# Layer 3 of a four-layer recurrent kernel: where the second pair's projections stand, and where the routing's one-hot rows live

## The chip, the cores and the metric

The kernel runs on one core of a Trainium2 chip (trn2), as a single program. The metric is the device time of one execution in microseconds (us); before the change the median of four runs is 1407.51 us (1401.19 to 1417.63). All arithmetic is fp32. The engines are named as the profile names them: PE (TensorE, matrix products), DVE (VectorE), ACT (ScalarE), POOL (GpSimd), and SP, which here only issues DMAs.

## The reference

The model has four layers. Each takes `x` (2 x 1024 tokens, 128 channels), normalises it, computes a mixer `s` and a mixture of experts `g` from the same normalised rows `xn`, and adds `s * silu(g)`:

```
xn = _layernorm(x)
s = _L3_attn_ref(xn, ...)          # two Mamba2 scans, one per direction, 64 channels each
g = _silu(_L3_ffn_ref(xn, ...))    # 16 experts of width 64, the best 2 per token, and a shared expert
x = x + s * g
```

Only layer 3 is touched. Its mixer runs a Mamba2 block forwards on the first 64 channels and one backwards on the last 64:

```
zxbcdt = u @ in_w.T
z, xBC, dt = ...
xBC = silu(conv4(xBC) + conv_b)                  # x, B and C, 128 columns each
dt = softplus(dt + dt_bias); dA = exp(-exp(A_log) * dt)
h = dA_t * h + outer(dt_t * x_t, B_t);  y_t = h @ C_t      # over 1024 steps, two heads of 64
y = rmsnorm((y + D * x) * silu(z)) * gnorm_w;  out = y @ outp_w.T
mixer(x) = x + concat(out_f, out_b) @ op_w.T + op_b        # here x is the layer's xn
```

Its experts choose, for each token, the two highest of 16 logits, weigh them by a softmax over the two, and add `down(silu(gate(xn)) * up(xn))` of the chosen two and of a shared expert.

## The kernel before

**Tiles.** The 2048 tokens are 16 tiles of 128 (`NT`), in four groups of four tiles (`NG`, `G`). `x`, `xn` (token rows) and `xT` (channel rows) stay in on-chip memory through the whole kernel. Layer 3 opens memory pools of its own: `pa` for the mixer, `pf` for the experts, `e3` for what comes after the routing, and eight PSUM banks, four for the mixer (`sa`) and four for the experts (`sf`).

**The mixer, `StateSpace`.** The scan is cut into chunks of 128 steps, and four chunks (512 tokens) of one direction are a *unit*. A forward and a backward unit are worked on together as a *pair*; there are four pairs. For each unit `stacked` makes the projections with the convolution folded in: three `px` (x, B, C; two matmuls of 128x512 accumulated in one bank each) that ACT turns into `uxs` by a Silu (line 473), and one `pz` that becomes `usz` (line 483). `xs` and `sz` have four buffers each, so two pairs' projections fit at once. `unit` then does the scan: decay matrices (`uda` on DVE or POOL, `pd` on PE, an exponential to `uE` on ACT, line 559), `pe`, the transposes `pt`, `pcb`, the states `pst`, then `py` and `pi`, the row norm (`pss`, `ur`) and the output product `pyo`, which `gated` (line 1736) adds into the tile `s0`. Between the two, `steps` makes the step sizes and decays for all tokens (a softplus on DVE with one exponential on ACT, line 344; then `pc` and the exponential of line 450).

**The experts.** `top2` finds the two experts of each token on DVE. The class `Dispatch` then works out, mostly on DVE, for each of 47 blocks of 128 rows which tokens go there: `pr` (a count by matmul), prefix sums, and at the end a list made by 32 small matmuls `pinv` of two kinds of one-hot rows: `dla`, made four tiles at a time in two buffers, and `dhh`, one tile of 128 x 1536 that DVE compares (line 1205) and POOL multiplies by the slot numbers (line 1206). The list gives `dfrom` and `dto`, for the gather of rows (line 1231) and the scatter of results (line 1241), both issued by POOL. The 47 blocks are worked on in twelve groups of four: gather `xb`, transpose `pxb`, `pgb`, Silu, `hb`, transpose `phb`, `pob`, copy to `yb`, scatter into `ys`. `xb` has two buffers, and the weights `tw` (issued by SP) three.

**The end.** When all scatters have landed, `fetch` reads `ys` back (`yt`) and DVE adds the rows to `acc` (line 409), which holds the shared expert's output (`pgt`, `put`, `hT`, `psh`). Then a Silu, the product with `s0`, the sum into `x`, and the store.

**What sets the order.** The program text gives an order of writing: normalisation, `top2`, `Dispatch`, `stacked` of pair 0, `steps`, units of pair 0 together with `stacked` of pair 1, the twelve expert groups, the shared expert, then for pairs 1 to 3 the units together with the next pair's `stacked`, then the end. The framework does not keep to it: it places the instructions on each engine by a timeline of its own (`schedule_with_timeline_sim=True`), in which what is written earlier has precedence. Each engine then works strictly in its own order and waits on semaphores. So one moved statement can move instructions of the experts on all engines.

**Where the one-hot rows live before.** `Dispatch` is given a place for `dhh`: a buffer of the tag `uxs` in `pa`, of 1536 elements, the first of the four that the projections use later. With pair 0 in the next two, the backward unit of pair 1 comes round to the buffer that held `dhh`.

Of the kernel before, what the change touches and what calls it, by code (L numbers as in the profile page):

```python
# [10 lines left out]
F32 = mybir.dt.float32  # L11
# [8 lines left out]
P = 128  # L20
NB, SEQ = 2, 1024
T = NB * SEQ
NT = T // P
# [630 lines left out]
def together(*parts):  # L654

    live = list(parts)
    while live:
        live = [p for p in live if next(p, p) is not p]
# [1000 lines left out]
def layer3(K, x, xn, xT, w, inp, out):  # L1659
    nc, tc, c = K.nc, K.tc, K.c  # L1660
    four = [P, G, P]
    with ExitStack() as es:
        pa = es.enter_context(tc.tile_pool(name="a3", bufs=1))
        pf = es.enter_context(tc.tile_pool(name="f3", bufs=1))
        sa = es.enter_context(tc.tile_pool(name="sa3", bufs=4, space=PSUM))
        sf = es.enter_context(tc.tile_pool(name="sf3", bufs=4, space=PSUM))
# [55 lines left out]
        with tc.tile_pool(name="r3", bufs=1) as pr:  # L1722
            lg = pr.tile([P, NT, 16], F32, name="lg")
            nc.vector.tensor_add(lg, pl[:, :, :16], w["br"].unsqueeze(1).to_broadcast([P, NT, 16]))
            pdt = pa.tile([P, NT, 4], F32, name="pdt")
            nc.vector.tensor_mul(pdt, pl[:, :, 16:], rs.unsqueeze(2).to_broadcast([P, NT, 4]))
            (m1, h1), (m2, h2) = K.top2(pr, lg, 16)
            d = Dispatch(K, pf, pr, sf, h1, h2, 16, P, inp["lists"], ((pa, "uxs", 4, 1536), (pa, "uda", 2)))
            w12 = K.pair_softmax(pf, m1, m2)
        pe = es.enter_context(tc.tile_pool(name="e3", bufs=1))  # L1730
        s0 = pa.tile([P, NT, P], F32, name="s")
        for g in range(NG):
            nc.gpsimd.tensor_add(grp(s0, g), grp(xn, g), w["opb"].unsqueeze(1).to_broadcast(four))

# [12 lines left out]
        space = StateSpace(K, pa, sa, parts)  # L1747
        pairs = [[(m, b, n) for m in parts] for b in range(NB) for n in range(TPB // G)]
        together(space.stacked(pairs[0]))
        space.steps(pdt)  # L1750
        together(*(space.unit(*u, busy=True) for u in pairs[0]), space.stacked(pairs[1]))
        loaded = {}

        def load_rows(n0):
# [5 lines left out]
        for n0 in range(0, d.n, 4):  # L1760
# [29 lines left out]
            K.copy(yb, po)  # L1790
            for r, n in enumerate(part):
                d.store(yb[:, r, :], n)
        acc = pe.tile([P, NT, P], F32, name="acc")
        for g in range(NG):
            rhs = xT[:, g * 512 : (g + 1) * 512]
            pgt = sf.tile([P, 512], F32, name="pgt", tag="ps")
# [21 lines left out]
def build(tc, io, packs):  # L1818
    nc = tc.nc
    with ExitStack() as ctx:  # L1820
        pool = ctx.enter_context(tc.tile_pool(name="const", bufs=1))
        x = pool.tile([P, NT, P], F32, name="x")
        src = io["x"].rearrange("b (t p) d -> p (b t) d", p=P)
        for g in range(NG):
            nc.sync.dma_start(grp(x, g), src[:, g * G : (g + 1) * G, :])
        xn = pool.tile([P, NT, P], F32, name="xn")
        xT = pool.tile([P, T], F32, name="xT")

        def load(into, n, by=nc.scalar):
            t = into.tile([P, packs[n].n], F32, name="w_" + n)  # L1830
            by.dma_start(t, io[n])
            return View(t, packs[n])

        K = Kern(tc, load(pool, "c"))
        dram = ctx.enter_context(tc.tile_pool(name="lists", bufs=1, space=DRAM))
        lists = {n: dram.tile([rows, P], F32, name=n) for n, rows in (("xs", T), ("ys", 2 * T))}
        views = {}
        with tc.tile_pool(name="const0", bufs=1) as pool0:
            w0 = load(pool0, "l0")
            e0 = load(pool0, "e0")  # L1840
            layer0(K, x, xn, xT, w0, e0)
        later = ctx.enter_context(tc.tile_pool(name="const3", bufs=1))
        views["l3"] = load(later, "l3")
        pair = lists["xs"], lists["ys"]
        with tc.tile_pool(name="const2", bufs=1) as pool0:
            views.update((n, load(pool0, n)) for n in ("l1", "l2"))
            layer1(K, x, xn, xT, views["l1"], {"rows": io["rows1"], "lists": pair, **{n: io[n] for n in ("sw1", "sw3", "sw2")}})
            layer2(K, x, xn, xT, views["l2"], {"rows": io["rows2"], "lists": pair})
        layer3(K, x, xn, xT, views["l3"], {"load": lambda pool: load(pool, "x3", nc.sync), "rows": io["rows3"], "lists": pair}, io["out"].rearrange("b (t p) d -> p (b t) d", p=P))
# [17 lines left out]
```

## Time and profile before

| what | us |
|---|---|
| median of 4 runs | 1407.51 (1401.19 to 1417.63) |
| the profiled execution, its own time | 1406.37 |
| its span | 1404.6 |
| busy in the span: PE, DVE, ACT, POOL | 1150.5, 878.0, 633.9, 430.9 |
| layer 3, from its first normalisation to the end of the span | about 1122 to 1404.6 |
| of which routing, until the list is ready | about 1152 to 1186 |
| pair 0, pair 1, pair 2 (from the first `pd` to the last `pyo`) | 1186 to 1245, 1245 to 1302, 1302 to 1351 |
| pair 3, the fetch and the end | 1351 to 1404.6 |

The median and the profiled execution differ by 1.1 us, and the four runs lie within 16.4 us of each other. In the views, a row of the timeline or the chain has the start in us from the span's start, then the duration, then the engine and what it writes; "issue" is time in which an engine waited for nothing that the profile shows. A PE row counts hardware passes: one fp32 matmul of the program is two of them. PEclk is the granted TensorE clock, 1.00 for full speed.

### The profile page before, as it was taken

What the parts mean: (1) busy time and instruction counts of PE and PEld (TensorE: products, weight loads), DVE (VectorE), ACT (ScalarE), POOL (GpSimd) and SP (SyncE); (2) the same over time, 40 slices, a digit from 0 to 9 for tenths busy, and PEclk for the clock granted to TensorE, in tenths of its full rate; (3) what the DMA queues carried; (4) which work ended last, traced back from release to release, by engine and by line L of the source; (5) the groups of instructions that cost most, each with busy time, mean ns of one, the idle gap of its engine ahead of it and who ended that gap; (6) DMA issues with size and microseconds to landing.
All of it is one profiled execution on the core that took longest, in us unless ns stands there. A gap on an engine that the chain in (4) does not pass through costs nothing. (4 is left out here: it accounts for less than half of the span.)

```text
span 1404.6 us, 19123 instructions
## 1 busy us (share of the span) xinstructions
PE 1150.5 (82%) x6813; PEld 801.4 (57%) x6813; DVE 878.0 (63%) x2169; ACT 633.9 (45%) x1051; POOL 430.9 (31%) x424
## 2 busy tenths in 40 slices
PE   5599776797997568999998997699999467887985
PEld 2276455796996335544444432377787344666674
DVE  6536336955754776777777635986673586434456
ACT  7656916116312241445556575225522243463561
POOL 0352260036555240000000000156575222655643
PEclk9799986889999776899999898889999767978997
DMA  2000003113443200000000000133345311222411
GB/s 87 0 1 1 0 15 119 46 43 122 133 132 100 60 1 0 1 1 1 1 1 16 8 1 8 74 83 113 127 133 153 95 58 53 69 62 82 56 51 45
DMA packets 49039, 75.71 MB, mean 54 GB/s; under 512 B 7335, under 2 KB 36402, under 8 KB 48688
## 3 DMA queue, kind: packets, MB, share of 16 engines
q1 hardware_dynamic: 39632, 54.30, 12.2%
q0 software_dynamic: 8448, 14.98, 4.6%
q10 hardware_dynamic: 864, 5.21, 1.0%
q8 instruction: 54, 0.88, 0.3%
q14 instruction: 41, 0.34, 0.1%
HBM read 63.95 MB, written 12.85 MB: 55 GB/s over the span
## 5 line engine op out<-in xcount | busy, mean ns | idle before, releaser
L1458 DVE TENSOR_REDUCE mx<-pm 128x1 f32<-128x512 f32 (+3 forms) x304 | 182.1, 656 | 65.6 <-PE pm L287 63.3
L1502 ACT ACTIVATE pr<-psc 128x1024 f32<-128x1024 f32 x144 | 139.5, 1021 | 94.8 <-PE psc L287 61.3
L1231 POOL DMA_INDIRECT xb<-xs,dfrom x132 | 132.5, 1004 | 150.7 <-PE pxb L808 30.9
L1241 POOL DMA_INDIRECT ys<-yb,dto x132 | 135.9, 1030 | 85.1 <-DVE yb L1119 33.5
L1206 POOL TENSOR_TENSOR dhh<-dhh,w_c 128x1280 fp32r<-128x1280 f32 (+2 forms) x3 | 8.7, 2915 | 474.3 <-DVE dhh L1205 474.3
L287 PE MATMUL pm<-kT,qT 32*128 32x128 f32 (+3 forms) x576 | 119.9, 367 | 16.3 <-DVE mx L1458 12.4
L287 PEld LDWEIGHTS pm<-kT,qT 32*128 32x128 f32 x576 | 69.6, 205 | 69.3 <-DVE mx L1458 49.3
L287 PE MATMUL p<-xbT,tw 128*128 128x256 f32 x368 | 103.1, 397 | 6.8 <-ACT sg L1112 2.4
L1112 ACT ACTIVATE sg<-p,tw 128x256 f32<-128x256 f32 x92 | 41.0, 473 | 100.3 <-PE p L287 85.8
L287 PE MATMUL pat<-pr,va 128*32 128x512 f32 x576 | 82.1, 637 | 0.2 <-ACT pr L1502 0.2
L293 PE MATMUL tp<-w_c,xn 128*128 128x128 f32 x64 | 19.5, 425 | 70.7 <-DVE xn L328 43.5
L287 PEld LDWEIGHTS p<-xbT,tw 128*128 128x128 f32 x368 | 63.8, 196 | 18.9 <-issue 6.4
L1113 DVE SCALAR_TENSOR_TENSOR hh<-p,tw,sg 128x256 f32<-128x256 f32 x92 | 42.6, 478 | 42.8 <-ACT sg L1112 22.0
L287 PE MATMUL psc<-qT,kT 32*128 32x512 f32 x288 | 64.3, 491 | 2.9 <-ACT pr L1502 2.7
L287 PEld LDWEIGHTS po<-tw,hh 128*128 128x128 f32 x368 | 54.3, 192 | 9.0 <-issue 2.2
L287 PE MATMUL po<-tw,hh 128*128 128x128 f32 x368 | 56.3, 277 | 1.0 <-DVE hh L1113 0.6
L293 PEld LDWEIGHTS tp<-w_c,xn 128*128 128x128 f32 x64 | 11.8, 191 | 78.7 <-DVE xn L328 27.8
L287 PE MATMUL psc<-mT,onesR 32*128 32x512 f32 x288 | 54.0, 415 | 0.0
L282 ACT COPY xbT<-pxb 128x256 f32<-128x256 f32 (+3 forms) x39 | 15.6, 400 | 66.2 <-PE pxb L808 34.9
L287 PEld LDWEIGHTS psc<-qT,kT 32*128 32x128 f32 x288 | 30.3, 188 | 15.9 <-ACT pr L1502 13.7
L287 PE MATMUL pd<-uda,w_c 128*128 128x512 f32 x64 | 38.4, 706 | 0.9 <-ACT usz L528 0.9
L556 POOL TENSOR_TENSOR uda<-w_c,vdA 128x512 f32<-128x512 f32 x20 | 20.9, 1053 | 55.4 <-PE pd L287 54.7
(529 smaller groups left out, 2851.1 us busy)
## 6 DMA issues: line engine op xcount, KB each, us to landing
tw<-in_rows SPq DMA_DIRECT2D x23, 836.0 KB
tw<-in_rows SPq DMA_DIRECT2D x39, 384.0 KB
yt<-ys SPq DMA_DIRECT2D x24, 256.0 KB
tw<-in_rows SPq DMA_DIRECT2D x47, 128.0 KB
xb<-xs,dfrom POOLq DMA_INDIRECT x132
ys<-yb,dto POOLq DMA_INDIRECT x132
xs<-xn SPq DMA_DIRECT2D x8, 256.0 KB
w_l<-in_l ACTq DMA_DIRECT2D x1, 1890.0 KB
```

Source lines behind the costliest of these rows:

```text
L282: self.nc.scalar.copy(out, in_)
L287: self.nc.tensor.matmul(out, lhsT=lhsT, rhs=rhs, start=start, stop=stop)
L293: self.nc.tensor.transpose(pt[:, j, :], src(g * G + j), self.c["ident"])
L556: pool.tensor_mul(da, upto.unsqueeze(1).unsqueeze(1).to_broadcast(lay), m["dA"][:, i0 + j : i0 + j + per, :].unsqueeze(3).to_broadcast(lay))
L1112: nc.scalar.activation(sg, p1[:, k - k0, :], AF.Silu, bias=t[:, 1536 + k : 1537 + k])
L1113: nc.vector.scalar_tensor_tensor(hh[:, k, :], p2[:, k - k0, :], t[:, 1540 + k : 1541 + k], sg, ALU.add, ALU.mult)
L1206: nc.gpsimd.tensor_mul(h, h.bitcast(F32), c["slot"][:, at].unsqueeze(2).to_broadcast(shape))
L1231: self.K.nc.gpsimd.indirect_dma_start(dst, None, self.xs, bass.IndirectOffsetOnAxis(self.of_token[:, n : n + 1], 0))
L1241: d = self.K.nc.gpsimd.indirect_dma_start(self.ys, bass.IndirectOffsetOnAxis(self.to[:, n : n + 1], 0), src, None, bounds_check=2 * T - 1, ...
L1458: nc.vector.tensor_reduce(mx[:, starts.index(a), g, j : j + k], tile[0][:, : k * m].rearrange("p (j m) -> p j m", m=m), AX.X, ALU.max)
L1502: K.nc.scalar.activation(pr, ps, AF.Exp, scale=scale)
```

## The change

Four edits, all in `layer3`:

```diff
-            d = Dispatch(..., ((pa, "uxs", 4, 1536), (pa, "uda", 2)))
+            d = Dispatch(..., ((pa, "acc", 1, T), (pa, "uda", 2)))
...
-        s0 = pa.tile([P, NT, P], F32, name="s")
+        s0 = xn
         for g in range(NG):
             nc.gpsimd.tensor_add(grp(s0, g), grp(xn, g), w["opb"].unsqueeze(1).to_broadcast(four))
...
         together(space.stacked(pairs[0]))
+        together(space.stacked(pairs[1]))
         space.steps(pdt)
-        together(*(space.unit(*u, busy=True) for u in pairs[0]), space.stacked(pairs[1]))
+        together(*(space.unit(*u, busy=True) for u in pairs[0]))
...
-        acc = pe.tile([P, NT, P], F32, name="acc")
+        acc = pa.tile([P, NT, P], F32, name="acc", tag="acc")
```

The projections of pair 1 are written right behind those of pair 0 and ahead of `steps`, instead of side by side with the units of pair 0. All four buffers of `uxs` then belong to the projections, and `dhh` gets a tile of its own, of 2048 elements, under the tag `acc`; the same tile later holds the experts' sum `acc`, which moves from the pool `e3` to `pa`. To make room, the separate tile `s` goes: the output bias is added to `xn` in place (POOL, line 1733), and the units add their output to `xn`. The arithmetic is the same.

More of the change, by code (lines that the diff above doesn't have):

```diff
@@ L1727, in layer3 @@
             (m1, h1), (m2, h2) = K.top2(pr, lg, 16)
-            d = Dispatch(K, pf, pr, sf, h1, h2, 16, P, inp["lists"], ((pa, "uxs", 4, 1536), (pa, "uda", 2)))
+            d = Dispatch(K, pf, pr, sf, h1, h2, 16, P, inp["lists"], ((pa, "acc", 1, T), (pa, "uda", 2)))
             w12 = K.pair_softmax(pf, m1, m2)
         pe = es.enter_context(tc.tile_pool(name="e3", bufs=1))
-        s0 = pa.tile([P, NT, P], F32, name="s")
+        s0 = xn
         for g in range(NG):
```

## The prediction

> **What bounds the kernel now.** I read the page, then the chain of work that ended last, the busy times by window, and the engines' own timelines for layer 3. Layers 0 to 2 keep their order, so only 1122 to 1404.6 us counts. The chain through the routing:
>
> ```profile
> 1150.71 22.93 issue
> ...
> 1173.68 3.15 POOL dhh L1206
> ...
> 1176.88 1.90 PE pinv L287 x8
> 1178.78 1.72 PE pc L287 x8
> 1180.50 5.36 PE pinv L287 x24
> ...
> 1185.88 3.75 PE pd L287 x4
> ```
>
> The chain waits 22.9 us for the routing's list of small DVE operations, then goes over POOL's `dhh` and PE's `pinv`. Windows of all engines (columns: PE, weight load, DVE, ACT, POOL busy, then the granted clock, DMA share, GB/s):
>
> ```profile
> 1158.00:1167.00 9.00, 8.81 (x24) 3.57 (x22) 7.54 (x39) 5.56 (x9) 0.00 (x0) 1.00 0.00 0
> 1167.00:1177.00 10.00, 0.12 (x1) 0.12 (x1) 9.86 (x21) 2.21 (x3) 3.14 (x1) 0.70 0.26 77
> 1177.00:1186.00 9.00, 8.98 (x41) 8.78 (x41) 5.32 (x9) 0.28 (x1) 0.00 (x0) 0.50 0.30 91
> ```
> ```profile
> 1186.00:1220.00 34.00, 33.10 (x154) 20.76 (x156) 15.45 (x34) 17.89 (x25) 20.91 (x20) 0.92 0.19 52
> 1220.00:1245.00 25.00, 17.03 (x109) 15.80 (x110) 9.42 (x24) 9.12 (x13) 14.49 (x16) 0.68 0.27 79
> ```
>
> PE stands idle for 10 us while DVE ends the routing, and is full (33.1 of 34) right after it. That is the place the change aims at: pair 1's projections stand in the full stretch and would go into the idle one. Their share of it, by the same view for `px` alone:
>
> ```profile
> 1186.00:1220.00 34.00, 12.02 (x24) 4.91 (x24) 0.00 (x0) 4.12 (x6) 0.92 0.19 52
> ```
>
> In the chain `px` takes 4.45 (1189.63), 3.44, 1.72 and 1.72 us, and `pz` 1.09: **12.4 us**, all on the path.
>
> **The change, part by part.** The sum is made against the profiled execution's own 1406.4 us; the median of the runs, 1407.5, lies 1.1 above it.
>
> *1. The routing gets later, its list shorter.* The built program's order puts pair 0's first Silu ahead of the softplus exponential `spe` on ACT. Before:
>
> ```profile
> 1153.25 1.28 ACT L344 ACT_TABLE_LOAD   x1
> 1155.02 0.26 ACT L344 ACTIVATE spe<-spe 128x64 f32<-128x64 f32 x1 [0.49 <-DVE spe L343]
> 1158.12 0.22 ACT L385 ACTIVATE rd<-rd 128x16 f32<-128x16 f32 x1 [2.85 <-DVE rd L384]
> 1158.36 1.28 ACT L473 ACT_TABLE_LOAD   x1
> ```
>
> Now `spe` waits for the first `px` (its row ends at 1156.3), a Silu (0.69) and a table load (1.28): it ends at 1156.4 + 0.7 + 1.3 + 0.3 = 1158.7 instead of 1155.3. Behind it on DVE waits line 345, and behind that all of `top2` and `Dispatch`; one reduction (0.42) now stands ahead, so DVE loses 2.9 us. The other exponential, `rd`, then stands behind a load, two Silus and a load (1.28 + 1.38 + 1.28 + 0.22): 1162.9, where DVE would want it at 1158.7 + 3.3 = 1162.0: 0.9 more. With five operations left to it (1.2 to 1.6), `dbo` ends near 1164.3, 4.1 late. The 2.1 us that DVE then waited for `pr` are filled now: step-size operations that stood among the prefix sums (lines 354, 444, 562: 0.9) run in that wait. That leaves `dhh` 3.2 late: `pinv` can begin at 1180, not 1176.9. The list itself gets shorter. `pc` (1.72) no longer cuts into it, because the new order has `pc` ahead. And at a granted clock of 1.00 its 32 matmuls (7.26 us at 0.50) are paced by six `dla` of 0.69 with a gap of 0.16: 5.1 + 0.5 = 5.6. End: 1185.6 at full clock, 1187.3 at half, against 1185.9. I take **+0.5**; bounds -2 (no exponential late) to +12 (rival two).
>
> A rule speaks against this part. The Trainium skill (ScalarE: Activation LUTs, "What ACT_TABLE_LOAD costs") puts a switch of tables at about 2.66 us, 1.28 for the load and 1.38 to drain. In this trace the Silu at 1194.18 ends at 1194.87, the load starts at 1194.89 and the exponential at 1196.18, so a switch costs 1.3 here. By the page's figure, an estimate, the three switches that now stand before `rd` would add 4 us to the routing.
>
> *2. Unit pair 0 loses 12.4 us of PE work.* Between `pinv`'s end (T0 = 1185.9) and the first `py` (1219.96) lie 34 us. What is late next is the first gather: POOL's four issues start 1.2 us after T0, stand 1.3 apart, and `pxb` now meets them with nothing but three `pd` (2.6 us at full clock) in front, so about 3 us of the hiding that `px` gave is lost; the rows are there at T0 + 5.6 (first two) and T0 + 8.8 (all). Then `xbT` and `uwide` on DVE (1.2), `pe` 0.9, `pt` and `pgb` with `pt` 2.7, `pcb` 1.8: T0 + 15.5. From `pcb` to `py` DVE decides: products, `hb`, `ucb`, `uE`, states, some 6.5 us: **T0 + 22 instead of T0 + 34, so -12**. From `py` to the last `pyo` (25 us) the work is like before. Bounds: -15 (everything that waited on PE moves up, full clock from T0 on, where `pd` ran at 0.54) to -6 (half of the freed time goes to waits on DVE and gathers).
>
> *3. The experts fall one group behind the units.* In the new order pair 0 takes three groups of gathers into its span instead of four, and the lag stays to the end: before, `pxb` and `pgb` of group twelve stand ahead of pair 2's `pyo`; now `pob` of group eleven and all of group twelve stand behind it. The rows before:
>
> ```profile
> 1347.44 3.62 PE pyo L287 x16
> 1351.07 0.64 PE phb L1783 x3
> 1351.71 1.92 PE pd L287 x4
> 1353.62 0.86 PE pob L287 x6
> ...
> 1360.73 2.67 DMA yt<-ys
> ```
>
> From `pyo` to the copy `yb` of group twelve (ends 1355.05) it was 4.1 us. Now: `pd` 0.86, `pob` 1.1, `pxb` 0.45, then (two `pd` beside it) ACT's `xbT`, `pgb`, three `uE`, a load 1.28 and the Silu 0.33 until 6.5, `hb` 0.35, `phb` 0.35, `hbT` 0.54, `pob` 0.87, `yb` 0.48, with waits 9.3; up to 12 at half clock. Scatters, fetch, `acc`, and on DVE everything of pair 3 that is queued behind `acc` hang on this. **+6**, bounds 0 to +8. The part of the lag that leaves pair 0 is inside the -12.
>
> *4. Fewer table loads.* The built order has 36 before and 27 after from the routing on: three more within the routing (priced above), twelve fewer later. On the chain they show in pair 1 as 3.8 us (1256.9 to 1262.5); four of that kind are still there, in other places. **-1.5**, bounds -8 to 0.
>
> *5. Homes.* `dhh`'s old buffer made the backward `uxs` of pair 1 wait for POOL, which was long done: nothing. `acc` is written 170 us after `dhh` was read: nothing. Adding the bias into `xn` makes POOL wait for the store of the rows to `xs` (issued 4 to 5 us before each addition), and `xw` of the next group stands behind it on POOL. Before, that copy waited for the addition in the other order (1137.76, where ACT had ended at 1136.7): between -1 and +3, I take nothing.
>
> Sum: 0.5 - 12 + 6 - 1.5 = -7: 1399.4 in the profiled execution, **1400** as a median.
>
> **The rivals.**
>
> *One, an episode goes.* In each of pairs 0 to 2, PE stops in the middle of `py`, and the clock then stays at half for some 12 us:
>
> ```profile
> 1225.18 7.49 another core or an unknown queue
> ...
> 1233.38 2.07 PE pob L287 x8
> ```
>
> The clock rows say 0.72 for 1226 to 1233 and 0.50 for 1233 to 1245; likewise 6.4 us from 1283.2, 3.6 from 1338.2. I can't tell their cause. If the new order spares one, it gives 7 and the lost half of 11.6 busy us, 6 more: 1387. For it: they all sit at one place of the order, which moves. Against: that place exists in the new order too.
>
> *Two, the projections become what the list waits for* (the change doesn't fill a gap, it moves one). They stand ahead of `pinv` on PE. At full clock their 24 passes of 0.43 take 10.3 us and `pz` 1.1, from 1165.8 to 1177.2, `pc` to 1178, ahead of `dhh` at 1180. At half clock (0.85 a pass, as `px` ran before 1158) they and `pc` end near 1190, 10 late, and the list takes 7.3 for 5.6: -7 + 11 = +4, 1411. Against: the clock was 1.00 from 1158, and they keep PE busy.
>
> *Three, slower: the thinner pair 0 runs at half clock.* PE's remaining busy time from T0 to `py` is 33.1 - 13.7 = 19.4 us; with the waits of step 2 in it, the clock may not rise at 1191.6 as before, nor hold. All of it at 0.50 costs 19 more, and the last group's 3: -7 + 22 = +15, 1422. It decides from about 7 us lost at half clock, where the gain is gone. The Trainium skill (TensorE: Matmul & The Clock Gate, "The HAM clock gate") says that half rate comes after one idle window of about 3.4 us; the rows above show 0.50 after 10 idle us, and no wait of mine in step 2 is as long as 3.4.
>
> **How the numbers follow.** My forecast (1393.4 to 1406) has 0.47; rival one, or more of step 2 and step 4 than I take (1383 to 1393.4), 0.26; rival two (1406 to 1414) 0.11; rival three, or an episode of 13 more (1414 to 1428), 0.16, most of it over 1421.6. The bounds of the four steps add to -25 and +14, and the rivals lie inside or just beyond them; the range, 1384 to 1421, leaves out the outer ends of both. One per cent is 14 us, about what a measurement of this kernel can tell from no change: faster gets 0.26, slower 0.13, and 0.61 lies between.
>
> **What would show it.** Right: `px` of pair 1 between `pr` and `pinv` at a clock of 1.00; `pinv` begins 2 to 4 us later but ends within 2 of 1186; first `py` some 22 us after; pair 2's `pyo` ends 12 to 16 earlier, and group twelve's `yb` only 5 to 9 earlier. Wrong: a half-clock row across pair 0, `pinv` waiting on `px` or `pc`, or the three stops changed in number.

## The result, and the profile after

The changed kernel took 1415.13 us (median of 44 runs) where the kernel before took 1410.87 (70 runs beside it): ratio 1.0015, 95% interval 0.9998 to 1.0031. No gain came; 0.5% was forecast. The ratio leaves out runs more than 1.5% above the fastest of their kernel (the medians alone give 1.0030), and as the first profile of the changed kernel, of 1420.99 us, is of such a run, the lines shown are from a later one, r17_after, of 1405.23 us (span 1403.4). It stands on a chip where before takes 1415, and is the fastest of its ten runs there (median 1412.75). Chips differ: on some the kernel before takes 1364 us, on others 1411 to 1421, so every ratio of an experiment is against runs of before on the same chip, and profiles are compared in pairs from one chip.

First the chain of work that ended last, through the routing and into pair 0 (start, us, what):

```profile
1178.36 3.16 POOL dhh L1206
...
1181.56 0.64 PE pinv L287 x4
...
1182.97 5.41 PE pinv L287 x24
...
1214.83 4.96 another core or an unknown queue
```

`pinv` still waits for `dhh`, which is late as forecast, and the list still ends when it did. The stop that rival one would have removed is still there (4.96 us). Windows over the end of the routing, all engines (PE, weight load, DVE, ACT and POOL busy, clock, DMA share, GB/s), and under them `px` alone (no column for POOL):

```profile
1160.00:1169.00 9.00, 9.00 (x22) 3.65 (x21) 7.45 (x35) 7.91 (x11) 0.00 (x0) 1.00 0.01 2
1169.00:1179.00 10.00, 10.00 (x25) 4.20 (x26) 9.72 (x33) 3.55 (x6) 0.64 (x1) 1.00 0.13 34
1179.00:1188.40 9.40, 8.49 (x45) 7.30 (x43) 7.81 (x8) 3.22 (x5) 2.51 (x1) 0.72 0.46 131
```
```profile
1169.00:1179.00 10.00, 9.85 (x23) 3.98 (x22) 0.00 (x0) 3.55 (x6) 1.00 0.13 34
```

PE was busy 0.12 us of the 10 in front of `pinv`; now it is busy all 10, nearly all of it with pair 1's `px`. The gap was filled. ACT's timeline there (start, us, line, operation):

```profile
1157.27 0.69 ACT L473 ACTIVATE uxs<-px,w_l 128x512 f32<-128x512 f32 x1 [0.64 <-PE px L287]
1157.97 1.28 ACT L344 ACT_TABLE_LOAD   x1
1159.27 0.26 ACT L344 ACTIVATE spe<-spe 128x64 f32<-128x64 f32 x1
...
1162.12 1.28 ACT L385 ACT_TABLE_LOAD   x1
1163.41 0.21 ACT L385 ACTIVATE rd<-rd 128x16 f32<-128x16 f32 x1
```

A Silu and a load stand ahead of `spe`, two switches ahead of `rd`, as the prediction had it.

The layer by stretches, in us, from two pairs of profiles, each pair on one chip. T0 is the end of `pinv`, a pair ends with its last `pyo`, and "twelfth `pob`" is the last product of the last group. The last two rows of the upper part are PE's idle time and its time at a granted clock of 0.50, from the trace's clock records:

| stretch | r18_before | r17_after | r15_before | r14_after |
|---|---|---|---|---|
| first `xn` to T0 | 57.1 | 57.3 | 56.7 | 56.4 |
| pair 0 | 61.5 | 43.8 | 44.4 | 34.6 |
| pair 1 | 57.1 | 60.4 | 44.5 | 48.0 |
| pair 2 | 48.5 | 52.3 | 44.2 | 42.5 |
| pair 3 | 47.2 | 51.8 | 48.1 | 51.4 |
| behind it | 6.7 | 6.7 | 6.7 | 6.7 |
| T0 to the twelfth `pob` | 170.7 | 165.6 | 138.3 | 134.2 |
| - PE idle in it | 21.8 | 31.3 | 6.4 | 9.2 |
| - at clock 0.50 | 45.5 | 32.5 | 4.3 | 11.3 |
| twelfth `pob` to the end | 50.3 | 49.4 | 49.5 | 49.0 |

Two things are seen. Pair 0 gets 10 to 18 us shorter, pairs 1 and 3 get 3 to 5 longer each, and pair 2 changes by -1.7 and +3.8. And the end follows the twelfth `pob` by 49.0 to 50.3 us in all four: in these, what moved that point moved the end.

### The profile page after: what moved, and what is told of

It reads as the page before. It is cut to its first block, busy times and chain, and to the rows that moved or that the text cites. A ratio compares the mean times of both kernels' runs of the same rounds, so it can differ in the third digit from the quotient of the medians.

```text
span 1419.1 us, 19118 instructions
## 1 busy us (share of the span) xinstructions
PE 1172.7 (83%) x6813; PEld 817.7 (58%) x6813; DVE 877.0 (62%) x2169; ACT 623.0 (44%) x1042; POOL 429.2 (30%) x424
## 5 line engine op out<-in xcount | busy, mean ns | idle before, releaser
L282 ACT COPY xbT<-pxb 128x256 f32<-128x256 f32 (+3 forms) x39 | 15.6, 399 | 72.5 <-PE pxb L808 34.9
L287 PE MATMUL pcum<-kv,w_c 128*128 128x512 f32 x64 | 34.1, 635 | 3.4 <-DVE prod L1322 3.0
```

The lines of the kernel that those rows point to most:

```text
L282: self.nc.scalar.copy(out, in_)
L287: self.nc.tensor.matmul(out, lhsT=lhsT, rhs=rhs, start=start, stop=stop)
```

## The experiments

My first theory was that pair 0's gain is real and that the twelve groups alone hold the end (theory 1). Its rivals: half clock eats the gain (theory 2), or the routing does (theory 3).

**The changed kernel again, and its parts.** r1_after is the changed kernel.

> The changed kernel itself, once more, for a profile that can be laid beside the one of before, and for its ratio. My first reading of the two profiles: the list of four ends about where it did counted from the first xn (+0.6 us), pair 0's units end 10 us earlier counted from it, and pairs 1 and 2 and the twelve groups give these 10 us back. Theory 1 (the end hangs on the experts' groups, which start when they did): pair 0's last pyo about 49 us behind pinv against 59, the twelfth yb no earlier than before (169 us behind pinv) or later, ratio 1.000 to 1.004. Theory 2 (the gain is eaten by stretches at half clock that the thinner pairs bring): the share of the layer at a granted clock of 0.5 is higher than before's in the same stretch by 10 us or more, and the pairs that lose are those with such stretches. Theory 3 (the routing itself ends late, and the profile at hand hid it): pinv ends 4 us or more later behind the first xn than before's 56.8.

Ratio 0.999 (0.9968 to 1.0013). The list ended 56.5 us behind the first `xn`, pair 0 34.8 behind T0, the twelfth `pob` 134.4. Theory 3 is out.

r2_home leaves the projections where they were and changes only the homes:

```diff
-        together(space.stacked(pairs[1]))
         space.steps(pdt)
-        together(*(space.unit(*u, busy=True) for u in pairs[0]))
+        together(*(space.unit(*u, busy=True) for u in pairs[0]), space.stacked(pairs[1]))
```

> Only the homes of the change (one-hot rows in the home of acc, s0 in xn's place, as in the changed kernel), with the second pair's projections left where they were, beside pair 0's units. Theory 1: pair 0 lasts as in the kernel before (about 59 us behind pinv) and the time is before's plus what the routing loses by the three removed and one added waits, +0.5 us: ratio 0.998 to 1.003. Theory 3 (the homes are dear and the projections pay for them): ratio 1.004 to 1.010, pinv ending 3 us or more later behind the first xn than before's 56.8, and the projections' move then has won what the homes lost.

Ratio 1.0002 (0.9978 to 1.0026), list at 56.8, pair 0 44.4. The homes cost nothing that can be measured here.

r3_move has the move with the homes of the kernel before:

```diff
-    ((pa, "acc", 1, T), (pa, "uda", 2))
+    ((pa, "uxs", 4, 1536), (pa, "uda", 2))
-        s0 = xn
+        s0 = pa.tile([P, NT, P], F32, name="s")
-        acc = pa.tile([P, NT, P], F32, name="acc", tag="acc")
+        acc = pe.tile([P, NT, P], F32, name="acc")
```

> Only the move: the second pair's projections directly behind the first pair's, with the homes of the kernel before (one-hot rows in the four rows of uxs). Here the projections' px stand between the four pinv instead of ahead of them. Theory 1: the 12 us that leave pair 0 are again given back by the groups; the px between the pinv put the list later by about their own 11 us, so that the sum is before's time or up to 8 us more: ratio 1.000 to 1.006. Theory 3: this kernel is faster than before by 4 us or more, since it has the move without the homes: ratio under 0.997.

Ratio 1.0041 (1.0019 to 1.0063). The list ended at 66.3, 9.6 late, since the `px` stand between the four parts of `pinv`; the twelfth `pob` came 134.3 behind T0. So the homes make the move possible at all: without a home of its own for `dhh`, the projections delay the list by more than they save behind it (9.6 us against the 4.0 that lie between 134.3 and r15_before's 138.3).

r4_between writes `steps` between the two projections:

```diff
         together(space.stacked(pairs[0]))
+        space.steps(pdt)
         together(space.stacked(pairs[1]))
-        space.steps(pdt)
```

> The changed kernel with one edit: the steps of the decay (steps, with its pdt) are written between the first pair's projections and the second's instead of behind both. Theory 1: within 0.2% of the changed kernel (ratio 0.999 to 1.004 against before). Theory 3: the steps' late place is what makes the routing late, and this kernel is faster than the changed one by 3 us or more, with pinv ending that much earlier behind the first xn.

Ratio 0.9988 (0.9963 to 1.0014), like the changed kernel. But in this profile the twelfth `pob` came 140.1 behind T0, with PE's matmuls behind the list the same, in the same order, as in r1_after, and 24.0 us at half clock instead of 11.6. All engines, T0 to the twelfth `pob`:

```profile
1172.90:1313.00 140.10, 130.80 (x789) 97.44 (x789) 76.00 (x178) 64.84 (x100) 98.69 (x96) 0.91 0.31 71
```

The same 789 passes took 125.0 busy us in r14_after, at a mean clock of 0.96.

**Without the groups.** r5_before is the kernel before, for a base on that chip (1418.3 us, pair 0 62.1 us):

> The kernel before, unchanged, for a profile beside the two that follow and for a second look at how its pairs lie: pair 0's last pyo 55 to 60 us behind the end of pinv by the first profile, 44 to 50 if the profile of the home edits alone (44.4) is the better guide on a chip like that one. Time within 1% of the other runs of before that stand beside it.

r6_before_noexp and r7_after_noexp leave the twelve groups out of both kernels, so that the output lacks the routed experts:

```diff
-        load_rows(0)
-        for n0 in range(0, d.n, 4):
-            ...
```

> The kernel before without layer 3's twelve groups of experts (no gathers, no pxb, pgb, phb and pob, no scatters; the fetch at the end adds whatever the layers before have left in the rows), so that only the mixer's four pairs stand behind the list. It is the base for the next run. Both theories: the tail behind pinv is shorter by 60 to 90 us than with the groups, since their PE work (12 groups of some 5 us) and their ACT and DVE copies go; ratio 0.93 to 0.96.

> The changed kernel with the same twelve groups left out. Theory 1 (the gain of pair 0 is real and only the groups hold the end): 8 to 12 us faster than the kernel before without the groups, that is a ratio to the full kernel before lower by 0.006 to 0.009 than that run's. Theory 2 (stretches at half clock, or the routing, eat the gain inside the mixer): no difference, ratios within 0.002 of each other.

Ratios 0.9551 (0.9506 to 0.9596) and 0.9495 (0.9453 to 0.9537); medians 1358.2 and 1347.54, so the change is worth 10.7 us without the groups, as theory 1 said. Its reason does not hold up in the trace, though. (The two profiled runs are the slowest of r6's six and the fastest of r7's, and differ by 11.0 us before layer 3 begins, so they show where time goes rather than how much.) From the first `xn` to the end the two profiles differ by 10.3 us; 4.1 of them come before T0, where another order puts the shared expert between the parts of `pinv` in both. Pair 0 gained only 4.0. Its windows (columns as above), before and changed:

```profile
1207.10:1250.10 43.00, 39.06 (x199) 26.54 (x199) 30.14 (x86) 24.81 (x34) 0.00 (x0) 0.93 0.16 47
```
```profile
1191.90:1230.90 39.00, 29.29 (x172) 23.48 (x172) 30.57 (x86) 23.01 (x29) 0.00 (x0) 0.85 0.19 54
```

PE lost 9.8 busy us there and stood idle 5.8 us longer, at a lower clock. Work taken from PE turns partly into waits even with no group in the way.

**Putting the work back.** If that is right (theory A), PE work added where the projections stood should come back as time, less where there are waits to hide it. A new function issues the second pair's matmuls once more, and nothing reads what they write (they do take their turns in the mixer's four PSUM banks). r8_after_fill has it in the changed kernel, r9_before_fill in the kernel before:

```diff
+    def filler(self, units):
+        ...
+                    K.mm(px, m["wx"][:, t, k * P : (k + 1) * P], cols[t], t == 0, t == 1)
+            ...
+            K.mm(pz, m["wz"][own, :P], cols[0][own])
...
-        together(*(space.unit(*u, busy=True) for u in pairs[0]))
+        together(*(space.unit(*u, busy=True) for u in pairs[0]), space.filler(pairs[1]))
```

> The changed kernel with PE work put back into pair 0 that nothing reads: the same 28 matmuls 128x512 (px, pz) of the second pair, a second time, beside pair 0's units. ACT and DVE get nothing more. PE's order then has the groups' pob 3, 4, 4 and 1 in the four pairs, like the kernel before, where the changed kernel has 2, 5, 3 and 2. Theory A (what stands now: the time follows PE's work ahead of the twelfth group, and half of what left pair 0 came back as waits of PE in the groups, 9 us of them against 4.5, since nothing covers those steps any more): the 12 us come back as 6 to 9 us of time, ratio 1.003 to 1.006, PE's idle time between pinv and the twelfth pob back at 4 to 5 us on a chip like that of the home edits, and the twelfth pob 138 to 142 us behind pinv. Theory B (PE's work in pair 0 was free, and something else sets the pitch of the groups): ratio 0.997 to 1.001, the twelfth pob 133 to 136 us behind pinv.

> The kernel before with the same 28 matmuls once more in pair 0, read by nothing. Theory A: PE has hardly any idle time to hide them in, so nearly all of their 12.4 us show: ratio 1.006 to 1.009, pair 0 longer by 10 to 12 us and the twelfth pob later by as much. Theory B: ratio 0.999 to 1.003.

In the kernel before they cost 14 us: ratio 1.0104 (1.0073 to 1.0135), more than I expected, with the twelfth `pob` at 149.6, 11.3 later than in r15_before. In the changed kernel the ratio to before is 1.0014 (0.9985 to 1.0043), below my 1.003, and 0.0024 above r1_after, a difference that the intervals do not separate from none. The trace is clearer: the twelfth `pob` at 141.4, 7.2 later than in r14_after. Here are both, T0 to the twelfth `pob`, first the changed kernel with the filler, then the kernel before with it:

```profile
1177.80:1319.20 141.40, 133.56 (x818) 95.69 (x817) 75.96 (x178) 64.64 (x100) 97.60 (x96) 0.98 0.30 70
```
```profile
1168.90:1318.50 149.60, 143.64 (x843) 99.50 (x843) 75.08 (x178) 83.52 (x118) 96.41 (x96) 0.98 0.28 66
```

With the filler the clock is 0.98, where r14_after had 0.96. The groups stood 2, 4, 4, 2 in the pairs, not 3, 4, 4, 1 as I had expected, so the filler does not restore the order of the kernel before.

**Another filling for the gap.** Since the end follows the twelfth `pob`, r10_shared puts the shared expert, which stands behind that point, into the gap, and leaves the projections in pair 0 (`xn` takes the place of `s` here too, to make room). r11_shared_busy adds the last pair's element-wise work on DVE:

```diff
             (m1, h1), (m2, h2) = K.top2(pr, lg, 16)
+            acc = pa.tile([P, NT, P], F32, name="acc")
+            for g in range(NG):
+                ...                                  # pgt, put, sg, hT, psh, the copy into acc, as before
...
-            together(*(space.unit(*u, busy=n < 2) for u in p), ...)      # r11_shared_busy alone
+            together(*(space.unit(*u, busy=True) for u in p), ...)
```

> What the runs so far point to: the end comes 49 to 51 us behind the twelfth group's pob in every profile, and the stretch in front of pinv has 15 us in which PE idles. So here the work that goes into that gap is the shared expert (pgt, put, psh: 16 matmuls 128x512 and 32 of 128x128, some 8.6 us of PE at full clock), which until now stands behind the twelfth pob, instead of the second pair's projections, which stay in pair 0. acc gets a home of its own, s0 takes xn's place, the one-hot rows go to uxs as in the kernel before. Theory A: the stretch behind the twelfth pob falls by 6 to 9 us, the list ends 0 to 4 us later since hT and the copies into acc stand on DVE in front of it, the rest is as before: 2 to 8 us faster, ratio 0.994 to 0.999. If the end is held by the last pair's own chain instead, the stretch behind the twelfth pob stays above 47 us: ratio 0.999 to 1.004.

> The same, and the last pair's element-wise work (uda, uwide, uxst, uE, uy) goes to DVE instead of POOL, as in the other pairs, since DVE no longer has hT and the copies of acc in that stretch. uy on POOL takes 1.26 us twice, where the same shape on DVE takes 0.7. Theory A: 1 to 3 us less than the run with the shared expert alone behind the twelfth pob. If DVE is what binds the last 20 us, 2 to 5 us more.

Ratios 1.0081 (1.0057 to 1.0106) and 1.0045 (1.002 to 1.0071): slower, against my 0.994 to 0.999. The list ended 64.9 us behind the first `xn`, 8.2 late (I had allowed 4), and the stretch behind the twelfth `pob` was 51.6, no shorter. So the shared expert was not what fills that stretch; the last pair's own chain is. With that pair's POOL work on DVE it fell to 44.4.

**The last pair on DVE.** r12_after_busy and r13_before_busy have that edit alone, in the changed kernel and in the kernel before. Theory C was that pair 3's `uda` on POOL holds up the last gathers in the changed kernel.

> The changed kernel with the last pair's element-wise work (uda, uwide, uxst, uE, uy) on DVE instead of POOL. In the changed kernel alone pair 3's uda stand on POOL ahead of the eleventh group's gathers and scatters. If that holds the groups up (theory C), the twelfth pob comes 2 to 5 us earlier behind pinv than the 134 to 140 of the profiles so far, and it is faster than the changed kernel by more than the kernel before gains from the same edit (ratio 0.993 to 0.996 against 0.998). Theory A (PE's order, its waits in the groups and its clock): the twelfth pob comes when it did, and what is gained is behind it, 49 us falling to 43 to 46, for uy's two steps on DVE and a DVE that is no longer slowed by POOL: ratio 0.994 to 0.998, as much as in the kernel before.

> The kernel before with the same edit. Theory A: the same 3 to 6 us behind the twelfth pob, ratio 0.995 to 0.998. Theory C: under 2 us, ratio 0.998 to 1.001.

> The changed kernel, for another profile: time at half clock between the end of pinv and the twelfth pob by theory A 14 us or more on a fast chip (over 8, the mean of the kernels that have the second pair's projections in pair 0) and 55 or more on one like that of the first profiles. PE's idle time in that stretch 4 to 5 us above that of the kernel before.

> The kernel before, for another profile on the same chip: half clock in the same stretch 5 to 11 us on a fast chip, 45 to 50 on one like that of the first profiles; idle time 4 to 6 us on a fast chip.

r12_after_busy: 0.9942 (0.992 to 0.9964), 1358.86 us against 1364.16. r13_before_busy: 1.0004 (0.9984 to 1.0024). Each theory missed by half: against C the twelfth `pob` came at 140.9, no earlier, and against A the kernel before gained nothing. Behind that point it is 41.9 us now against 49.0, and only together with the move. The plain profiles beside them missed too: r14_after had 11.3 us at half clock (I had expected 14 or more) and 2.9 us more idle time than r15_before (4 to 5); r15_before had 4.3 and 6.4 (5 to 11, and 4 to 6). PE's timeline shows what the edit did. First r14_after, then r12_after_busy, then r13_before_busy (in brackets: idle time before the row, and what ended it):

```profile
1307.26 0.83 PE L287 MATMUL pgb<-tw,xbT 128*128 128x128 f32 x6
1310.24 0.52 PE L1784 MATMUL phb<-w_c,hb 128*64 128x128 f32 x3 [2.15 <-DVE hb L1781]
1311.40 0.93 PE L287 MATMUL pob<-tw,hbT 64*128 64x128 f32 x6 [0.64 <-DVE hbT L284]
```
```profile
1310.15 0.83 PE L287 MATMUL pgb<-tw,xbT 128*128 128x128 f32 x6
1310.81 1.02 PE L287 MATMUL pd<-uda,w_c 128*128 128x512 f32 x2
1311.67 1.05 PE L287 MATMUL pe<-w_c,uwide 128*128 128x128 f32 x8
1313.12 0.52 PE L1784 MATMUL phb<-w_c,hb 128*64 128x128 f32 x3 [0.40 <-DVE hb L1781]
1313.59 1.13 PE L287 MATMUL pe<-w_c,uwide 128*128 128x128 f32 x8
1314.55 1.47 PE L578 MATMUL pt<-w_c,uxs 128*128 128x128 f32 x12
1315.95 0.93 PE L287 MATMUL pob<-tw,hbT 64*128 64x128 f32 x6
```
```profile
1310.27 0.93 PE L287 MATMUL pob<-tw,hbT 64*128 64x128 f32 x6 [1.62 <-DVE hbT L284]
...
1314.67 1.05 PE L287 MATMUL pe<-w_c,uwide 128*128 128x128 f32 x8
```

With the last pair's element-wise work on DVE, its `pe` and `pt` stand inside group twelve and fill the waits between its steps; the pair is that much further when the group ends. In r13_before_busy all `pe` and `pt` of the pair stay behind the twelfth `pob`. That the framework moves them only in the changed kernel was seen, not explained. From r14_after to r12_after_busy the profiles themselves show hardly a gain: the end came 7.1 us sooner behind a twelfth `pob` that came 6.7 us later (4.0 for the work that now stands ahead of it, 5.2 for more time at half clock, less 2.4 of idle time). The gain is in the medians of the runs.

The same version, the changed kernel and the kernel before on a chip of the slower sort:

> The changed kernel with the last pair's element-wise work on DVE, again. If the gain (0.994) comes from what stands behind the twelfth pob, it is there whatever the chip: ratio 0.992 to 0.997, and 4 to 8 us faster than the changed kernel beside it. If it came from that run's clock alone: ratio 0.998 to 1.003.

> The changed kernel, again. On a chip where before takes 1364 us: ratio 0.997 to 1.000, time at half clock between pinv and the twelfth pob 11 or 24 us (the two amounts that its profiles have shown so far). On a chip where before takes 1410 us or more: ratio 1.000 to 1.004, half clock in that stretch 55 us or more.

> The kernel before, for a profile beside these two: half clock in that stretch 4 to 11 us where before takes 1364 us, 45 to 50 us where it takes 1410 us or more.

r16_after_busy: 0.9943 (0.991 to 0.9976), 1409.5 us against 1415.11; r17_after: 0.9989 (0.9949 to 1.0028). In r16_after_busy too the end came 41.9 us behind the twelfth `pob`. So this version is faster than the kernel before on both sorts of chip, by 5.3 and 5.6 us. Against the changed kernel it is less clear: 3.3 us less by the medians here, where I had expected 4 to 8, with intervals that overlap; on the faster sort its 0.9942 lies below r1_after's 0.999, measured on another chip. r17_after missed both of its expectations: ratio below 1.000, and 32.5 us at half clock instead of 55 or more. r18_before had 45.5, within its 45 to 50.

## Why the prediction was wrong

**Where the twelve microseconds went.** The matmuls that leave the stretch between T0 and the twelfth `pob` are, at full clock, 24 `px` passes of 0.43, four `pz` (1.1), less two `pd` (0.9) that now stand ahead of that point: 10.5 us. (The 12.4 us of the prediction, read from the chain, had some of these matmuls at half clock.) Each us at half clock loses half of itself, and new idle time adds. PE's time is the sum of these three, so the sum has to close; what the table shows is their sizes. From r15_before's 138.3 it closes to 0.5 us in five profiles on faster chips:

| profile | work | half clock / 2 | idle | sum | measured |
|---|---|---|---|---|---|
| r14_after | -10.5 | +3.5 | +2.8 | 134.1 | 134.2 |
| r4_between | -10.5 | +9.9 | +2.9 | 140.6 | 140.1 |
| r12_after_busy (16 `pe`, 12 `pt`, two `pd` more) | -6.5 | +8.7 | +0.4 | 140.9 | 140.9 |
| r8_after_fill (two `pd` more) | +0.9 | +0.3 | +1.4 | 140.9 | 141.4 |
| r9_before_fill | +11.4 | +0.3 | -0.4 | 149.6 | 149.6 |

On the slower chip, from r18_before to r17_after, the terms are -10.5, -6.5 and +9.5: 163.2 against 165.6 measured. There 13.5 us of the idle time are three stops in front of `py`; r18_before has 13.8 to 15.6 in stops of that kind, so the growth is in the smaller waits.

The waits are in the groups' steps. PE's waits in that stretch (waiting for whom: us in total, times, longest), r15_before, then r14_after:

```profile
PE pob L287 <- ACT hbT L282: 2.2, 3, 0.7
PE pob L287 <- DVE hbT L284: 1.6, 1, 1.6
PE px L287 <- DVE s L1736: 1.2, 2, 0.7
```
```profile
PE phb L1784 <- DVE hb L1781: 3.9, 4, 2.1
PE pgb L287 <- ACT ut L638: 1.7, 2, 0.8
PE pgb L287 <- ACT yb L282: 1.0, 1, 1.0
PE pxb L1772 <- DMA xb<-xs,dfrom: 0.8, 2, 0.5
```

In both kernels the longest single wait (1.6 and 2.1 us) is in group twelve. Its row in r14_after stands above (`phb`); in r15_before it is

```profile
1307.33 0.93 PE L287 MATMUL pob<-tw,hbT 64*128 64x128 f32 x6 [1.62 <-DVE hbT L284]
```

The waits for `hb` and for ACT's queue appear at the same sizes in r1_after, r3_move and r4_between, those for the gathers (0.8 and 1.0) in r1_after and r4_between.

**Point by point.**

- *Step 1, +0.5: right.* Measured from the first `xn`, `dhh` began 2.3 later (45.4 against 43.1; 1.6 on the faster chip), `pinv` took 6.8 us instead of 9.0, and the list ended +0.2 and -0.3. The switches of tables cost what the trace had said: 1.31 us from the end of the Silu to `spe` (1157.96 to 1159.27). By the 2.66 us of the Trainium skill (ScalarE: Activation LUTs, "What ACT_TABLE_LOAD costs"), `spe` would have come at 1160.6; the measurement decides.
- *Step 2, -12: the step that failed.* Pair 0 did lose 10 to 18 us, and the first `py` came 19.5 (26.0 on the slower chip) behind T0, 11 to 13 earlier. But I carried the whole -12 to the end of the kernel but for step 3, and wrote that "from `py` to the last `pyo` the work is like before": for idle time and half clock behind the first `py` the sum has nothing. The groups ended 2, 5, 3 and 2 to a pair instead of 3, 4, 4 and 1. Part of what left pair 0 was a group put off into pair 1 (+3.3 and +3.5 there), and what had covered the groups' steps was gone (+2.8 to +9.5 of idle time). Counted from the first `xn`, pair 2's last `pyo` came 8.3 and 10.4 us earlier (12 to 16 was forecast) and `yb` of group twelve 4.5 and 5.0 (5 to 9). At the twelfth `pob` 4 to 5 us were left of the 12.
- *Step 3, +6: nearly right.* `yb` of the twelfth group ended 9.6 behind pair 2's last `pyo` (9.3 was forecast) where it had been 4.2, and 5.8 on the faster chip: +5.4 and +3.8. Pair 3 grew by 4.6 and 3.3.
- *Step 4, -1.5: the count was right* (36 loads before, 27 after); no run separated its gain.
- *Step 5, 0: right* (r2_home, 1.0002).
- *Rivals.* One did not come: the stops stayed. Two did not come either, and r3_move shows when it does: list 9.6 late. Three named a mechanism that is there at a smaller size: in the table 3.5 to 10 us more are lost at half clock in the kernels with the move and no filler, not 19, and 7 was where it decides. In all profiles of kernels with the projections in pair 0 on faster chips (r2_home, r9, r10, r11, r13, r15) the time at half clock between T0 and the twelfth `pob` was 4 to 13 us; with the move (r1, r3, r4, r12, r14) 10 to 24.

So the profiles of the changed kernel have a layer 3 that is 5.1 us (r14_after) and 5.8 us (r17_after) shorter than before's, near my -7; the medians show -2.5 and -2.4 us on two chips and +4.3 in the first comparison. Two things in the record bear on the difference. r17_after's 6.5 us from less half clock belong to the fastest of ten runs. And r4_between, with PE's order behind the list the same, got 24.0 us at half clock where r1_after and r14_after got 11.6 and 11.3: 6 us of time, more than the gain.

The granted clocks of all runs allow an estimate of the mean run, since 2 x (1 - clock) x time is the time at half clock. Over the whole kernel it is 303 us in the changed kernel and 306 before on r1_after's chip, 348 and 358 on r17_after's (standard errors of the differences 4 and 5). From the first `xn` to T0 the changed kernel has 17.5 and 13.4 us less of it (25.6 against 43.1 in r14_after and r15_before, 30.0 against 43.4 in r17_after and r18_before). If layers 0 to 2 do not differ, some 14 and 4 us more then lie behind T0, which cost 7 and 2. With -10.5 for the work and +2.8 and +9.5 for idle time that makes about -1 and +1, which the medians of those two chips do not contradict within these errors. So on the one chip half clock, on the other idle time would take most of the gain. This is an estimate and not shown, and why the first comparison stands at +4.3 stays open: of before's runs there only one has its clock on record.

Which amount at half clock an execution gets is not settled either. The Trainium skill (TensorE: Matmul & The Clock Gate, "Part 1: The HAM clock gate") says that the gate watches windows of 3.4 us that run freely, whatever the kernel does; the trace agrees in so far as the spells last multiples of 3.41 us. That the phase of these windows decides is not borne out: counted from the starts of the spells, the list ends 2.03 and 2.34 us into a window in r1_after and r14_after, and 2.17 and 2.26, between the two, in r4_between and r12_after_busy, which got twice the half clock.

## What to carry to other kernels

Work moved from a full stretch of an engine into an idle one is worth its busy time only if the stretch that it leaves stays full: ask what stood behind it waiting, and count the waits that it covered. Find the point that the end follows at a fixed distance (here the twelfth `pob`, 49 to 50 us), and carry each saving to that point rather than to the end of the stage where it arises. Here the best version put other ready work into some of the new waits: with the last pair's element-wise work on DVE, the changed kernel ran at 0.994 of before, while the same edit did nothing for the kernel before (1.0004). And compare the whole set of runs, not the profiled ones: ahead of layer 3, which the change does not touch, the profiles from the faster chips already have between 222 and 253 us at half clock.

## What the hardware showed that I had not expected

- Two sorts of chip, 1364 and 1411 to 1421 us for one kernel. Between T0 and the twelfth `pob`, before took 138.3 and 170.7 us, with 4.3 and 45.5 us at half clock and 6.4 and 21.8 us of idle PE; the stops "another core or an unknown queue" (0.7 to 7.5 us, two to six on the chain in layer 3) are in the profiles before, r5_before, r16_after_busy, r17_after and r18_before from the slower sort and in none of the twelve from the other. r6_before_noexp and r7_after_noexp, on r5_before's chip but without the groups, have none, so as far as these two show they need the groups' work. Their cause stays open.
- DVE waits for POOL. The same operations of the last pair's stretch, r15_before and then r13_before_busy, where POOL has only the scatters:

```profile
L409 DVE SCALAR_TENSOR_TENSOR acc<-yt,rw,acc 128x128 f32<-128x128 f32 x16 | 6.6, 469 | 2.6 <-DMA yt<-ys 2.6
```
```profile
L409 DVE SCALAR_TENSOR_TENSOR acc<-yt,rw,acc 128x128 f32<-128x128 f32 x16 | 4.4, 342 | 2.4 <-DMA yt<-ys 2.4
```

  The Trainium skill (SBUF — State Buffer, "SBUF: two separate sides") says that the two share a pair of ports which one instruction holds to its end. The trace agrees: in r15_before three of these operations took 595, 1126 and 1350 ns, each began while a product of POOL (`uxst` or `uE`) ran and ended 0.15 us after it did, and the other thirteen took 339 to 351 ns.
- In these single profiles the changed kernel kept its clock better with useless work on PE: 0.98 with the filler, 0.96 and 0.91 in r14_after and r4_between without.
